# One layer with a state-space scan and a routed feed-forward: another order inside the inner layer's banks, a margin for ScalarE, and one name set right

## The chip, the cores and the metric

The kernel runs on one core of a Trainium2 chip. Its engines are TensorE (matmuls and transposes, PE; its weight loads are shown as PEld), VectorE (DVE), ScalarE (ACT), GpSimd (POOL) and SyncE (SP, which issues the transfers here). Each engine works through its own queue in the order of the program, and waits at an instruction until its operands are ready. The metric is the device time of one execution in microseconds; lower is better.

## What is computed

Input u has 4 sequences of 2048 tokens with 256 features. All arithmetic is in float32.

```
x = u + ssm(layernorm(u))
out = x + ffn(layernorm(x))

ssm: u_in = v @ W_in.T + b_in; x, z = halves (512 channels each)
     delta, B, C from x @ W_x.T (rank 16, 16 states, 16 states); delta = softplus(delta @ W_dt.T + b_dt)
     h[t] = h[t-1] * exp(delta[t] * A) + x[t] * delta[t] * B[t]       per channel and state
     y[t] = sum over states of h[t] * C[t];  y = (y + x * D) * silu(z);  y @ W_out.T + b_out

ffn: scores = softmax(v @ Wg.T + bg) over 4 experts, the best two are kept, with weights w
     h_e = relu(v @ Wi.T + low-rank part of expert e)       (1024 features)
     out = sum over the two of w_e * (h_e @ Wo.T)
```

## The kernel before

The 8192 tokens are cut into 16 chunks of 512. For a chunk there are 512 channels in 4 blocks of 128 and 16 states, so 64 scans of a 128x512 tile; 1024 scans in all are the backbone of the program. One scan takes:

- on ScalarE a decay `dA = exp(delta * a)`, made two scans ahead, and a small copy of the last column (`carry`) for the next chunk;
- on GpSimd `dBx = xdt * B` for two states at once, four scans ahead (`xdt` is delta times x);
- on VectorE the scan itself (a tensor_tensor_scan), and a product `hC = h * C`. For every fourth scan this product is made on GpSimd and called `hP`;
- on TensorE four transposes that add `hC` into the bank of y.

Everything else is put between the scans: the front of the next chunk (layer norm, projections `pin`, `pdbc`, `pdt`, their copies `xT`, `dbc`, `delta`, the softplus over delta, then `xdt`), the gate (`g`, a silu), the output projection of the last chunk (`po`), and the last chunk's feed-forward, here called the inner layer.

The inner layer of a chunk has 8 halves k (4 token blocks, 2 halves of 512 features). A half has one PSUM bank `pz`. Two matmuls with x2T (`p_base`, line 661; four records in the profile) give the part that all experts share. `p_low` (line 670) adds the low-rank part: in one step, the second slot's part of half k, and the first slot's of half k-1. The first slot's operand is the difference of the two experts' masks, so it turns the bank from one expert to the other. `a_relu` (line 681) reads the bank twice, first with slot 1 and then, after the next `p_low`, with slot 0, and gives the bank back. `p_hT` transposes and sums the two relus, ScalarE copies `hT`, and `p_down` (`pf`) projects it down.

The order is not written out by hand. `Pacer` (line 45) holds threads of `Step`s. A step has an engine, a cost in us, the steps it comes after, and PSUM banks that it takes or gives back (three banks in all, for everything but y and dA). The pacer keeps a planned time for each engine. After each scan and after each read, `fill` (line 106) writes out the side steps that are `ready` (line 126). For ScalarE a step is ready when its planned start is at most 0.6 us after VectorE's planned time and its end at most 1.5 us, or when it could have begun 0.5 us earlier. `force` (line 147) writes a step, and all it needs, at once; the main loop does so at deadlines. After the last scan `drain` (line 138) writes what is left, in order of planned start.

`front` gives back a chunk's `xdts`, the steps that make delta times x. The first chunk's are named `xdts` in line 897. In the main loop line 954 sets the same name to the next chunk's; line 952 uses it at scan 27.

All instructions are recorded through a helper in line 30, so the profile names line 30 for nearly all of them; the tiles' names tell them apart.

Of the kernel before, what the change touches and what calls it, by code (L numbers as in the profile page):

```python
# [44 lines left out]
class Pacer:  # L45
# [80 lines left out]
    def ready(self, x):  # L126
        t = self.start(x)
        if t is None:
            return False
        v = self.now["dve"]  # L130
        if self.quiet and x.engine == "act" and x.cost > self.MOST:
            return False
        if x.engine == "dve":
            t = max([y.end for y in x.after if y.engine != "dve"], default=0.0)
            return t + self.LATENCY + self.MARGIN <= v
        return t <= v + self.BEGIN[x.engine] and (t + x.cost <= v + self.END[x.engine] or t <= v - 0.5)

    def drain(self):
# [30 lines left out]
def ssm_moe_layer_kernel(  # L169
# [100 lines left out]
    bm_sb = const.tile([32 * TOPK, F], F32, tag="bm_sb", name="bm_sb")  # L270
# [18 lines left out]
    def mm_tile(name):  # L289
        return ps.tile([P, TC], F32, tag="mm", name=name)  # L290

    pe, act, dve, pool = (InOrder(tc, e) for e in (nc.tensor, nc.scalar, nc.vector, nc.gpsimd))
    pacer = Pacer(BANKS)
# [83 lines left out]
    def new_xnT(c):  # L377
        st[c]["xnT"] = chunk.tile([P, KM, TC], F32, tag="xnT", name=f"xnT_{c}", bufs=1)
        return st[c]["xnT"]
# [5 lines left out]
    def front_norm(c):  # L385
        def load():
            if c + 1 < NCHUNK:
                us[c + 1] = load_u(c + 1, "ua")

        return layernorm_T(lambda: us[c], lambda: new_xnT(c), f"a{c}", Step("sp", 5.0, load))  # L390
# [167 lines left out]
    def ffn(c):  # L558

        s = st[c]  # L560
        q = {}
# [96 lines left out]
        HF = F // 2  # L658
        NK = 2 * NJ

        def p_base(k):
            j, half = divmod(k, 2)
            pm = q["z", k] = mm_tile(f"pz_{c}_{k}")
            for m in range(KM):
                pe.matmul(
                    pm, lhsT=s["x2T"][:, m, j * P : (j + 1) * P], rhs=wi_sb[:, m, half * HF : (half + 1) * HF],
                    start=(m == 0), stop=False, skip_group_check=True,
                )

        def p_low(k):  # L670
            for slot, x in ((1, k), (0, k - 1)):
                if 0 <= x < NK:
                    j, half = divmod(x, 2)
                    r = slice(32 * slot, 32 * slot + ER)
                    pe.matmul(
                        q["z", x], lhsT=s["lowT"][r, j * P : (j + 1) * P],
                        rhs=bm_sb[r, half * HF : (half + 1) * HF], start=False, stop=True,
                        skip_group_check=True,
                    )

        def a_relu(k, slot):
            h = q["h", k, slot] = work.tile([P, HF], F32, tag=f"h{slot}", name=f"h{slot}_{c}_{k}")
            act.activation(h, q["z", k], AF.Relu, scale=s["topv"][:, slot, k // 2 : k // 2 + 1])
# [36 lines left out]
        steps = layernorm_T(lambda: s["u"], lambda: new_x2T(c), f"f{c}")  # L720
# [14 lines left out]
        last = steps[-1]  # L735
        for x in steps[-3:]:
            x.after = [steps[steps.index(x) - 1]] + held.get("low", [])
        z1s, hs, copies = [], [], []
        bases = [Step("pe", 1.75, lambda k=k: p_base(k), after=[last], takes=1) for k in range(NK)]
        steps.append(bases[0])  # L740
        for k in range(NK + 1):

            low = Step(
                "pe", 1.06 if 0 < k < NK else 1.05, lambda k=k: p_low(k), after=bases[k : k + 1] + z1s[-1:]
            )
            steps.append(low)
            if k:
                hs.append(Step("act", 0.57, lambda k=k: a_relu(k - 1, 0), after=[low], gives=1))
                steps.append(hs[-1])
            if k < NK:  # L750
                z1s.append(Step("act", 0.57, lambda k=k: a_relu(k, 1), after=[low]))
                steps.append(z1s[-1])
            steps += bases[k + 1 : k + 2]
            if k:
                steps.append(Step("pe", 0.88, lambda k=k: p_hT(k - 1), after=[hs[-1]], takes=1))
                steps.append(Step("act", 0.5, lambda k=k: a_hT(k - 1), after=[steps[-1]], gives=1))
                copies.append(steps[-1])
            for j in range(NJ):
                if k == min(2 * j + 3, NK):
                    for h in range(2):  # L760
                        steps.append(
                            Step("pe", 1.75, lambda j=j, h=h: p_down(j, h), after=[copies[2 * j + 1]], takes=1 - h)
                        )
                    steps.append(Step("dve", 0.33, lambda j=j: add(j), after=[steps[-1]], gives=1))
# [6 lines left out]
    def load_bc(i, h):  # L771
# [11 lines left out]
    states = [  # L783
        (c, (c * NH + hf) * NG + g, hf * ND2 + dd, g * NN + k)
        for c in range(NCHUNK) for hf in range(NH) for g in range(NG) for dd in range(ND2) for k in range(NN)
    ]
# [107 lines left out]

    spare = small.tile([P, 1], F32, tag="spare", name="spare", bufs=1)
    act.activation(spare, mhalf[:, 0:1], AF.Softplus)
    f, g, dbc, xdts = front(0, front_norm(0))
    pacer.add(f)
    pacer.force(f[2 * NJ])
    join_x()  # L900
# [4 lines left out]
        load_bc(i, 0)  # L905
    for i in range(2):
        load_bc(i, 1)
    pacer.force(xdts[0])

    act.activation(a_sb, a_sb, AF.Exp)  # L910
    dve.tensor_scalar_mul(a_sb, a_sb, -1.0)
    pacer.add(g)
    for i in range(0, AHEAD_B, NN):
        pacer.force(xdts[states[i][2]])
        X[i] = X[i + 1] = pacer.run("pool", 2.32, lambda: enter(i))
    for i in range(AHEAD_A + 1):
        A[i] = pacer.run("act", 0.63, lambda: decay(i))
# [6 lines left out]
    for i in range(M + 4):  # L924

        pacer.quiet = (i + 5) % (PER // NH) < 8
        if turn:
            pacer.run("pe", 0.45, *turn)
            turn = None
        for e in (1, 4):  # L930

            if i + e < M + 3 and i + e >= 3:
                c, _, d, n = states[i + e - 3]
                c2, d2 = (c + 1, d - ND2) if d >= ND2 else (c, d + ND2)
                if n == N - 1 and e == (1 if d % ND2 else 4) and c2 < NCHUNK:
                    scale, x = open_y(c2, d2)
                    xds[c2, d2] = x, [pacer.run("act", 0.63, scale)]
        if 3 <= i < M + 3:
            c, _, d, n = states[i - 3]
            if n == N - 1:  # L940
                copy, *steps = close_y(c, d)
                pacer.force(silus[c])
                steps[0].after = [pacer.run("act", 0.5, copy, [Y[i - 3]]), silus[c]]
                pacer.add(steps, first=True)
                gates.setdefault(c, []).append(steps[-1])
                turn = xds.pop((c + 1, d - ND2) if d >= ND2 else (c, d + ND2), None)
                if d == ND - 1:
                    begin(c + 1)
        if i < M:
            at = i % PER  # L950
            if i == PER // NH - AHEAD_B - 1:
                pacer.force(xdts[-1])
            if states[i][0] + 1 in deadline:
                dbc, xdts = deadline[states[i][0] + 1]
                if at == PER - 3 * NN * ND2 - 2:
                    pacer.force(dbc)
                if at == PER - AHEAD_B - 6:
                    pacer.force(xdts[0].after[0])
                if at == PER - AHEAD_B - 1:
                    pacer.force(xdts[-1])  # L960
            S[i] = pacer.run("dve", 1.2 if states[i][0] % CPB else 1.14, lambda: scan(i), [A[i], X[i]])
        if i + AHEAD_B < M and i % NN == 0:
            X[i + AHEAD_B] = X[i + AHEAD_B + 1] = pacer.run(
                "pool", 2.32, lambda: enter(i + AHEAD_B), [S[i - 1]]
            )
        pacer.fill()

        if 1 <= i <= M:
            if shared(i - 1):
                C[i - 1] = pacer.run("pool", 1.23, lambda: read(i - 1), [S[i - 1]])  # L970
            else:
                C[i - 1] = pacer.run("dve", 0.6, lambda: read(i - 1), [S[i - 1], *summed[-4:-3]])
            pacer.run("act", 0.1, lambda: keep(i - 1), [(S if shared(i - 1) else C)[i - 1]])
            if i + AHEAD_A < M:
                A[i + AHEAD_A] = pacer.run(
                    "act", 0.63, lambda: decay(i + AHEAD_A), [(S if shared(i - 1) else C)[i - 1]]
                )
        for late in (3, 2):
            if late <= i < M + late and (late == 3) == shared(i - late):
                Y[i - late] = pacer.run("pe", 0.45, lambda: sum_y(i - late), [C[i - late]])  # L980
                if late == 2:
                    summed.append(Y[i - late])
        if i < M:
            group(i)
        pacer.fill()
# [48 lines left out]
```

## Time and profile before

| | us |
|---|---|
| median of 3 runs | 2129.7 (2126.46 to 2132.01) |
| profiled execution | 2129.43 |
| its span | 2127.7 |
| VectorE busy | 1855.8 |
| TensorE busy | 1873.9 |
| GpSimd busy | 1709.4 |
| ScalarE busy | 1441.7 |
| mean granted TensorE clock | 0.929 |

The span is the time from the first to the last instruction of the profiled execution; 1.7 us of its time lie around it. A row of a group or of the timeline gives line, engine, operation, output<-inputs and shape; a number in square brackets, with an arrow, is the idle time of the engine just before and what ended it. Some matmul records can be missing, and a group of matmuls overlaps with the next by the pipeline, so that its time is a little longer than from start to start.

### The profile page before, as it was taken

How to read it: one execution, taken by the hardware profiler on the slowest of the kernel's cores; microseconds unless marked ns; L12 is line 12 of the kernel's file. 1: busy time of each engine (PE TensorE's matmuls, PEld its weight loads, DVE VectorE, ACT ScalarE, POOL GpSimd, SP SyncE). 2: the span in 40 equal slices, each digit the busy share in tenths (PEclk: the TensorE clock that was granted, in tenths of full speed). 3: DMA queues.
4: the chain of work that ended last, by engine and by line, in shares of the span. 5: the costliest groups of instructions: out<-in, count | busy, mean ns of one | idle time of the engine just before them, and what ended most of it. 6: DMA issues, size and time to landing. Idle time of an engine off the chain costs nothing.

```text
span 2127.7 us, 28591 instructions
## 1 busy us (share of the span) xinstructions
PE 1873.9 (88%) x9504; PEld 1284.0 (60%) x9504; DVE 1855.8 (87%) x2423; ACT 1441.7 (68%) x2898; POOL 1709.4 (80%) x1084
## 2 busy tenths in 40 slices
PE   7768788998889989899899988989899998989978
PEld 4445555665566665657666565766657575666655
DVE  4899898999989989999989998999989999999810
ACT  5857667667676667676767777676677867766522
POOL 5898888989878878888888888888888888878600
PEclk9859799998999999999999999999999999989989
DMA  7454344445444443434435454444535444444200
GB/s 218 144 165 152 127 150 149 149 147 161 151 139 151 149 140 138 169 130 149 163 130 164 140 167 132 147 152 139 169 130 173 136 141 149 138 149 140 98 10 10
DMA packets 106132, 300.70 MB, mean 141 GB/s; under 512 B 12864, under 2 KB 39104, under 8 KB 105984
## 3 DMA queue, kind: packets, MB, share of 16 engines
q1 hardware_dynamic: 105984, 298.88, 42.8%
q8 instruction: 74, 1.21, 0.2%
q14 instruction: 74, 0.61, 0.1%
HBM read 289.41 MB, written 9.44 MB: 140 GB/s over the span
## 4 chain that ended last, share of the span: by engine, by line
PE 25%; DVE 20%; ACT 12%; issue 5%; POOL 1%; DVEq 0%; POOLq 0%; ACTq 0%
DVE dA L30 9%; PE pz L30 9%; PE y L30 5%; PE pf L30 5%; ACT dA L30 5%; DVE hC L30 4%; DVE hS L30 4%; PE phT L30 3%; ACT L30 2%; ACT h L30 1%; PE pin L30 1%; ACT delta L30 1%; ACT g L30 1%; DVE u L30 1%; DVE plg L30 1%
## 5 line engine op out<-in xcount | busy, mean ns | idle before, releaser
L30 POOL TENSOR_TENSOR dBx<-xdt,B 128x1024 f32<-128x1024 f32 x512 | 1207.8, 2363 | 187.5 <-DVE dA L30 157.3
L30 ACT ACTIVATE dA<-delta,a_sb 128x512 f32<-128x512 f32 x1024 | 706.8, 693 | 143.0 <-DVE hC L30 66.8
L30 DVE TENSOR_TENSOR_SCAN dA<-dA,carry,dBx 128x512 f32<-128x512 f32 x576 | 726.4, 1279 | 62.6 <-ACT dA L30 51.0
L30 PE MATMUL y<-ident,hC 128*128 128x128 f32 x3072 | 490.7, 291 | 36.6 <-DVE hC L30 36.5
L30 DVE TENSOR_TENSOR hC<-dA,C 128x512 f32<-128x512 f32 x768 | 514.1, 670 | 0.2 <-issue 0.2
L30 PEld LDWEIGHTS y<-ident,hC 128*128 128x128 f32 x3072 | 386.1, 150 | 181.3 <-issue 73.6
L30 POOL TENSOR_TENSOR hP<-hS,C 128x512 f32<-128x512 f32 x256 | 326.6, 1276 | 5.1 <-issue 4.1
L30 PE MATMUL pz<-wi_sb,x2T 128*128 128x512 f32 x512 | 271.7, 657 | 25.2 <-ACT hT L30 15.4
L30 DVE TENSOR_TENSOR_SCAN dA<-dA,dBx 128x512 f32<-128x512 f32 x192 | 231.2, 1220 | 35.3 <-ACT dA L30 30.5
L30 DVE TENSOR_TENSOR_SCAN hS<-dA,carry,dBx 128x512 f32<-128x512 f32 x192 | 244.1, 1271 | 18.6 <-ACT carry L30 10.6
L30 PE MATMUL pf<-wo_sb,hT 128*128 128x256 f32 x1024 | 243.4, 383 | 11.6 <-ACT hT L30 9.4
L30 PE MATMUL pin<-xnT,w_in_sb 128*128 128x512 f32 x512 | 245.9, 612 | 5.5 <-ACT g L30 3.6
L30 ACT COPY carry<-dA 128x1 f32<-128x1 f32 x576 | 90.1, 157 | 208.5 <-DVE hC L30 206.5
L30 ACT ACTIVATE h<-pz,topv 128x512 f32<-128x512 f32 x256 | 165.4, 680 | 74.1 <-PE pz L30 73.4
L30 PEld LDWEIGHTS pf<-wo_sb,hT 128*128 128x128 f32 x1024 | 186.5, 190 | 41.6 <-ACT hT L30 14.4
L30 PEld LDWEIGHTS y<-ident,hP 128*128 128x128 f32 x1024 | 128.3, 148 | 96.3 <-issue 56.7
L30 PE MATMUL y<-ident,hP 128*128 128x128 f32 x1024 | 167.1, 288 | 18.7 <-POOL hP L30 18.7
L30 PEld LDWEIGHTS pz<-wi_sb,x2T 128*128 128x128 f32 x512 | 95.2, 207 | 124.9 <-issue 76.2
L30 PE MATMUL pz<-bm_sb,lowT 16*128 16x512 f32 x512 | 167.9, 660 | 0.0
L30 PE MATMUL phT<-ident,h 128*128 128x128 f32 x1024 | 139.7, 281 | 21.3 <-ACT h L30 16.8
L30 PEld LDWEIGHTS pin<-xnT,w_in_sb 128*128 128x128 f32 x512 | 92.3, 197 | 93.1 <-issue 75.2
L30 PEld LDWEIGHTS phT<-ident,h 128*128 128x128 f32 x1024 | 120.8, 145 | 44.2 <-ACT h L30 19.5
(94 smaller groups left out, 1784.8 us busy)
## 6 DMA issues: line engine op xcount, KB each, us to landing
B<-bc SPq DMA_DIRECT2D x256, 512.0 KB, 3.7
C<-bc SPq DMA_DIRECT2D x256, 512.0 KB, 3.7
ua<-in_u_dram SPq DMA_DIRECT2D x16, 512.0 KB, 5.5
u<-in_u_dram SPq DMA_DIRECT2D x16, 512.0 KB, 4.4
out_dram<-u SPq DMA_DIRECT2D x16, 512.0 KB, 4.8
w_in_sb<-in_w_inT_dram SPq DMA_DIRECT2D x2, 512.0 KB, 4.7
wi_sb<-in_wiT_dram SPq DMA_DIRECT2D x1, 1024.0 KB, 6.7
wo_sb<-in_woT_dram SPq DMA_DIRECT2D x1, 1024.0 KB, 10.4
```

The source lines that it names most:

```text
L30: return self._tc.keep_in_program_order(f(*args, **kwargs))
```

## The change

Three things are changed.

- In the inner layer a bank is begun by the second slot's low-rank part (`start=True`), then the base is added, then the relu of slot 1 reads it; the first slot's part still comes last. `p_low` of half k takes the bank, `p_base` of half k comes after it, and the relu of slot 1 comes after the base.
- A ScalarE step that comes after a TensorE step whose planned end is close is ready only when ScalarE's planned time has reached that end (and that end plus 0.5 us lies at most 0.6 us after VectorE's planned time). For such a step the rule on its own end no longer applies.
- The first chunk's `xdts` have a name of their own, `first_xdts`, and line 952 uses that.

```diff
@@ Pacer.ready
             return t + self.LATENCY + self.MARGIN <= v
+        if x.engine == "act" and any(y.engine == "pe" and y.end + 0.5 > t for y in x.after):
+            t = max(y.end for y in x.after) + 0.5
+            return t <= v + self.BEGIN["act"] and self.now["act"] + 0.5 >= t
         return t <= v + self.BEGIN[x.engine] and (t + x.cost <= v + self.END[x.engine] or t <= v - 0.5)
@@ p_base
-            pm = q["z", k] = mm_tile(f"pz_{c}_{k}")
+            pm = q["z", k]
...
-                    start=(m == 0), stop=False, skip_group_check=True,
+                    start=False, stop=True, skip_group_check=True,
@@ p_low
                 if 0 <= x < NK:
+                    if slot:
+                        q["z", x] = mm_tile(f"pz_{c}_{x}")
...
-                        rhs=bm_sb[r, half * HF : (half + 1) * HF], start=False, stop=True,
+                        rhs=bm_sb[r, half * HF : (half + 1) * HF], start=bool(slot), stop=not slot,
@@ ffn
-        bases = [Step("pe", 1.75, lambda k=k: p_base(k), after=[last], takes=1) for k in range(NK)]
-        steps.append(bases[0])
+        bases = []
...
-                "pe", 1.06 if 0 < k < NK else 1.05, lambda k=k: p_low(k), after=bases[k : k + 1] + z1s[-1:]
+                "pe", 1.06 if 0 < k < NK else 1.05, lambda k=k: p_low(k), after=[last] + z1s[-1:], takes=int(k < NK)
...
             if k < NK:
-                z1s.append(Step("act", 0.57, lambda k=k: a_relu(k, 1), after=[low]))
-                steps.append(z1s[-1])
-            steps += bases[k + 1 : k + 2]
+                bases.append(Step("pe", 1.75, lambda k=k: p_base(k), after=[low]))
+                z1s.append(Step("act", 0.57, lambda k=k: a_relu(k, 1), after=bases[-1:]))
+                steps += [bases[-1], z1s[-1]]
@@ start and main loop
-    f, g, dbc, xdts = front(0, front_norm(0))
+    f, g, dbc, first_xdts = front(0, front_norm(0))
...
-    pacer.force(xdts[0])
+    pacer.force(first_xdts[0])
...
-        pacer.force(xdts[states[i][2]])
+        pacer.force(first_xdts[states[i][2]])
...
             if i == PER // NH - AHEAD_B - 1:
-                pacer.force(xdts[-1])
+                pacer.force(first_xdts[-1])
```

## The prediction

> **What bounds the kernel now.** I read the page's busy shares first, then busy time by stage, then VectorE's waits, then single stretches in order of time.
>
> ```profile
> PE 1873.9 (88%) x9504; PEld 1284.0 (60%) x9504; DVE 1855.8 (87%) x2423; ACT 1441.7 (68%) x2898; POOL 1709.4 (80%) x1084
> ...
> 43.00:151.00 108.00, 75.33 (x321) 48.50 (x319) 96.81 (x115) 74.91 (x156) 96.45 (x56) 0.73 0.49 160
> ...
> 647.00:2015.00 1368.00, 1250.23 (x6515) 863.80 (x6514) 1271.66 (x1654) 969.25 (x1960) 1164.57 (x733) 0.95 0.44 146
> 2015.00:2054.00 39.00, 37.69 (x182) 26.69 (x180) 5.07 (x10) 9.86 (x16) 0.00 (x0) 1.00 0.04 14
> 2054.00:2072.00 18.00, 6.47 (x25) 5.14 (x26) 4.79 (x22) 4.41 (x11) 3.11 (x10) 0.56 0.00 0
> 2072.00:2128.00 56.00, 49.58 (x196) 28.34 (x196) 1.70 (x4) 15.51 (x25) 0.00 (x0) 0.96 0.03 10
> ```
>
> The columns of a stage are span, PE, PEld, DVE, ACT and POOL busy, granted clock, DMA share, GB/s. From 43 to 2015 the 1024 scans run: VectorE is the fullest engine (1271.66 of 1368 in the long stage). From 2015 no scan is left and TensorE alone works: that is the drain, 113 us. So the time is the scan stream plus the drain, and the stream can shrink only by VectorE's idle time. What it waits for between 43 and 2015:
>
> ```profile
> DVE dA L30 <- ACT dA L30: 79.6, 128, 6.1
> DVE hS L30 <- ACT carry L30: 21.0, 10, 6.5
> DVE hS L30 <- ACT dA L30: 7.8, 8, 1.5
> ```
>
> Nearly all is ScalarE (108.4 us in these three rows): a decay exp(delta*a) comes late, because something stood ahead of it in ScalarE's queue. ScalarE's own waits in the same window say what:
>
> ```profile
> ACT hT L30 <- PE phT L30: 61.9, 62, 3.9
> ACT h L30 <- PE pz L30: 40.7, 53, 3.7
> ```
>
> ScalarE has slack (969 of 1368 busy), so it is the order of its queue that hurts. I went through every VectorE gap of 0.3 us or more in the stream, looking at the last ScalarE instructions before it. They sum to 118 us: 56 us behind a pack with two table loads (softplus or silu), 39 us behind a copy or relu that waited for TensorE (h, hT, xT, g, delta and the like), 14 us behind the copies of y and the next chunk's xd, 9 us other. Three of the packs stand out; this is the longest, VectorE's gap and ScalarE meanwhile:
>
> ```profile
> 626.72 1.22 DVE L30 TENSOR_TENSOR_SCAN hS<-dA,dBx 128x512 f32<-128x512 f32 x1 [6.45 <-ACT carry L30]
> ```
>
> ```profile
> 620.08 1.27 ACT L30 ACTIVATE delta<-pdt,b_dt_sb 128x512 f32<-128x512 f32 x2 [1.25 <-PE pdt L30]
> 621.36 1.28 ACT L30 ACT_TABLE_LOAD   x1
> 622.65 1.91 ACT L30 ACTIVATE delta<-delta 128x2048 f32<-128x2048 f32 x1
> 624.47 0.14 ACT L30 COPY carry<-dA 128x1 f32<-128x1 f32 x1
> 624.63 1.28 ACT L30 ACT_TABLE_LOAD   x1
> ```
>
> Four delta copies, a wait and the softplus pack stand between two decays. Gaps of this kind: 6.07 (89.99), 6.45 (626.72) and 3.60 us (754.77).
>
> **The change, part by part.** The number of instructions, of table loads (64) and of transfers is the same; only the order differs. I read it from both programs, counting by scan.
>
> (a) The first chunk's xdts. Line 954 sets the name xdts to the second chunk's steps from scan 0 on, so line 952 at scan 27 does not find the first chunk's, and forces the whole front of chunk 1. That is the 6.07 us gap. In the changed program nothing is forced at 27, and that softplus stands at scan 36. The gaps at 626.72 and 754.77 are forces at deadlines (scans 310 and 374); in the changed order no force does anything any more after the start, since the softplus of those chunks comes at scan 35 and 26 of the chunk, in place of 54. All 31 softplus and silu packs then have the ordinary size: pack, one carry, one decay, 5.3 us of ScalarE work, against 7.4, 8.0 and 6.7 for the three forced ones (copies times their rows). A softplus that is not forced cost VectorE 0.6 us in the mean over 12 chunks (0 to 2.3). Gain: 6.07 + 6.45 + 3.60 - 3 x 0.6 = 14 us. Ends: 7 (each ends up beside a silu pack, which costs some 2 us) and 16. The silu packs stay (about 2 us each, 31 us).
>
> (b) The margin. A step after a TensorE step is now put into ScalarE's queue only when ScalarE's planned time has reached the planned end. In the changed order a relu stands 1.57 scans behind its matmul in the mean, before 1.16; a copy of hT 1.71, before 1.12; xT and g 1.56, before 0.92. One scan with its read and its share of side work is 1972 / 1024 = 1.93 us, so they come 0.8 to 1.2 us later. The gaps they cause are 39 us in some 40 pieces, about 0.9 us each: by size alone most would go. Not all: the longest ScalarE waits are 3.7 and 3.9 us, and what waits behind a later relu is the bank and the next low-rank step. What is late next is the copy of y, which is not asked with a margin (14 us stays), and the packs. Ends: 32 saved, and a loss of 20 (rival below). By the size of the pieces I would take 23.
>
> Here a rule of the Trainium skill stands against the change. The row first: low-rank matmuls take 1.13 us for a group of four, and 2.08 at 1072.77, just ahead of a relu that waited 1.46 us and a VectorE gap of 1.64; a base group took 1.98 us in the drain, and 3.62 at 2072.75 after 18 us at a granted 0.56. "TensorE: Matmul & The Clock Gate" (Part 1, the HAM clock gate) says that the array goes to half speed after an idle window of about 3.4 us and needs as long a busy one to come back. The long stage's 0.95 is then 10% of its time at half speed, 43 to 151 at 0.73 more than half. Until now the first relu of a bank waited for the low-rank pair, which half speed makes 0.95 us longer; from now on it waits for the base group, 1.6 us longer, and the margin is 0.5. By the rows at full clock the sum has 23; by the rule, 10% of 120 first relus lose up to 0.7 us more, 8 us on ScalarE, of which perhaps a third reaches VectorE. I take 20.
>
> (c) The bank. Before: base(k+1) ran while relu 1 of bank k ran. After: low(k), base(k), hT(k-1), low(k+1); low(k+1) needs relu 1 of k (0.69 us, and 0.18 from the matmuls' end to the relu, as at 2019.36 and 2019.54 in the drain), and hT(k-1), 0.96 us, lies in between. Cost in the stream: nothing, covered by hT; without that cover 0.9 us per bank. Behind a low(k+1) that waits stand, on TensorE, the sums of y, which free VectorE's four hC buffers; VectorE's read waited 0.2 us in all before, so two or three scans of delay there cost nothing. On POOL and SP the moved steps are xdt (1.27 us each, 4 per chunk), the layer norms' small steps and one load of u (5.5 us to land, asked a chunk ahead): they move with their fronts by some ten scans, and VectorE waited 3.9 us for POOL in the whole stream. I take nothing for them, 5 us without that cover.
>
> (d) The drain. Because everything of chunk 14's inner layer comes later, more of it is left: in the changed order 7 bases instead of 3, 8 hT groups instead of 5, 7 low groups instead of 5, 8 half down-projections instead of 6. In rows (start to start in the drain): 4 x 1.82 + 3 x 0.96 + 2 x 1.05 + 2 x 1.82 = 15.9 us of TensorE. Not all of it lengthens the path. Before the layer norm of chunk 15 stand 7 bases (12.7), 6 low (6.3), 7 hT (6.7), py (1.7), two down pairs (7.3) and po (7.0): 41.7 us against the 35.3 from 2018.3 to 2053.6, +6.4; the rest (a down pair, low 8, hT, the last down pair) now fills the 18 us in which TensorE had 6.47 busy, and lengthens those by perhaps 1.5 (relu 8 ahead of xn, a half down-projection ahead of the routing). The last sums of y no longer stand behind a down pair (2012.90 to 2016.62): -1.6. The last inner layer begins with the low-rank part, so its base is not under the copy of lowT: +1.82, less the 1.0 to 1.5 that before lost at other waits: +0.5. Sum +6.8, ends 2 and 14.
>
> Sum against the profiled execution (span 2127.7, 1.7 us around it, 2129.4; the median of the runs is 2129.7, the same): -14 - 20 + 7 = -27, so 2102.5 us.
>
> **The rivals.**
> Half gain. The packs, not TensorE, set ScalarE's lateness, and the waits only move to the copies of y: (a) 9, (b) 8, (d) +11: 2123.5. For it: 56 us of packs and 14 of y stay. Against: the order by scans moves every kind of step.
> Slower: the first relu now waits for the base. Place: relu 1 of 120 banks. If TensorE is later than planned (hC sums take 0.60 to 0.66 us in the rows, planned 0.45), each such relu waits 0.5 us longer and half reaches VectorE, (b) turns into +30: -14 + 30 + 7 = 2152; with 0.3 us, +18, 2140. It decides from +7, that is 0.06 us per relu on VectorE; 2136 and more need 0.12. For it: ScalarE waits 40.7 us for pz already. Against: relus stand 0.4 scan later.
> The change doesn't do what it says: that nothing is forced any more is seen in the order, so (a) is only open in size, and this has little weight.
>
> **How the numbers follow.** A run of this kernel can tell some 0.3%, 6.4 us, from no change. Forecast 0.60 (2085 to 2115), half gain 0.20 (2115 to 2130), slower 0.20 (2130 to 2152). Faster by over 0.3% (below 2123.3): 0.60 and half of half gain, 0.70. Same: the other half and a tenth of the slower case, 0.12. Slower: 0.18. Lowest end: -16 - 32 + 2 = -46, 2083. Range 2080 to 2140: the low end with a little below it, the high end into the slower case at 0.3 us per relu.
>
> **What would show it.** Right: no VectorE gap over 4 us behind a softplus; ScalarE's waits for pz and phT in the stream below 60 us together (102.6 before); VectorE idle in the stream down by 25 to 40; the last scan at about 1980 and a drain of about 120 us. Wrong: ScalarE's wait for pz grows, or the drain grows by over 15 us, or VectorE waits for sums of y (hC <- PE).

## The result, and the profile after

The changed kernel takes 2111.0 us (median of 4 runs, 2109.3 to 2111.8) against 2130.6 (4 runs, 2126.5 to 2132.0): a ratio of 0.991, 95% interval 0.990 to 0.992. It is faster by 19.6 us, three times the 6.4 us that the prediction took as the least that can be told. The forecast was 2102.5, so 8.5 us of the forecast gain are missing. The profiled execution took 2109.27 us, its span is 2107.5.

The same stages as before, cut where the new execution has its edges. The first row is the page's, the others are busy time by stage (span, PE, PEld, DVE, ACT and POOL busy, granted clock, DMA share, GB/s):

```profile
PE 1860.5 (88%) x9504; PEld 1266.0 (60%) x9504; DVE 1852.9 (88%) x2423; ACT 1440.0 (68%) x2898; POOL 1707.3 (81%) x1084
...
43.00:151.00 108.00, 75.75 (x328) 49.55 (x326) 99.95 (x118) 75.73 (x158) 100.76 (x58) 0.70 0.50 169
647.00:1984.00 1337.00, 1213.27 (x6365) 832.93 (x6366) 1255.02 (x1631) 954.76 (x1925) 1150.26 (x723) 0.95 0.45 148
1984.00:2031.00 47.00, 46.52 (x212) 29.67 (x211) 4.82 (x10) 15.48 (x24) 0.00 (x0) 0.99 0.00 0
2031.00:2049.00 18.00, 12.70 (x67) 9.39 (x65) 5.23 (x24) 5.31 (x13) 3.10 (x10) 0.93 0.09 30
2049.00:2108.00 59.00, 53.36 (x193) 29.92 (x192) 1.70 (x4) 16.26 (x25) 0.00 (x0) 0.88 0.03 9
```

VectorE works as long as before, and the scans end at 1984 instead of 2015. The first drain stage is 47 us and was 39, TensorE full in both; the 18 us of the layer norm and routing now hold 12.70 us of TensorE's work, before 6.47; the last stage is 59 for 56, at a granted 0.88 for 0.96. From the first scan's start to the last one's end the stream went from 1983.2 to 1952.4 (-30.8), the drain from 112.9 to 123.4 (+10.5).

What VectorE waits for in the stream (its three largest rows), then ScalarE's waits for `pz` and `phT`, whose rows of before stand in the prediction (total, times, longest; us):

```profile
DVE dA L30 <- ACT dA L30: 71.6, 122, 2.4
DVE hS L30 <- ACT carry L30: 13.9, 12, 2.3
DVE dA L30 <- ACT carry L30: 7.5, 6, 3.1
```

```profile
ACT h L30 <- PE pz L30: 40.2, 56, 3.0
...
ACT hT L30 <- PE phT L30: 4.0, 13, 0.6
```

The longest wait of VectorE for a decay or a carry is 3.1 us, where three forced packs made 6.45, 6.07 and 3.60. ScalarE's wait for `phT` fell from 61.9 to 4.0 us. The one for `pz` did not fall at all: 40.7 before, 40.2 now. That is the first thing to explain.

VectorE's gaps of 0.3 us and more in the stream (all but the one ahead of the first scan), put down to the last things that ScalarE did before each, as in the prediction, beside the drain (us). A pack is a softplus or silu with its two table loads; PE-fed steps are copies and relus that waited for TensorE. Where several of these stand before one gap the class is a choice: another count of the last instructions moves the entries of before and of the changed kernel by up to 3 us, those of E3 to E5 by up to 7. Sums and drains don't depend on it.

| kernel | packs | PE-fed steps | copies of y, xd | other | sum | drain |
|---|---|---|---|---|---|---|
| before | 56.3 | 38.6 | 14.2 | 8.7 | 117.8 | 112.9 |
| after | 42.2 | 20.8 | 17.9 | 10.5 | 91.4 | 123.4 |
| before + name (E1) | 51.5 | 31.1 | 14.6 | 9.4 | 106.6 | 112.9 |
| before + margin (E2) | 53.2 | 11.9 | 10.1 | 19.7 | 94.9 | 130.8 |
| before + bank order (E3) | 60.7 | 58.0 | 14.1 | 8.2 | 141.0 | 102.4 |
| after - bank order (E4) | 50.0 | 7.4 | 10.1 | 22.4 | 89.9 | 131.0 |
| after - margin (E5) | 56.6 | 59.0 | 14.3 | 8.2 | 138.1 | 102.4 |
| after - name (E6) | 47.9 | 20.7 | 18.4 | 10.5 | 97.6 | 119.7 |

### The profile page after: what moved, and what is told of

It reads as the page before. It is cut to its first block, busy times and chain, and to the rows that moved or that the text cites. A ratio compares the mean times of both kernels' runs of the same rounds, so it can differ in the third digit from the quotient of the medians.

```text
span 2107.5 us, 28645 instructions
## 1 busy us (share of the span) xinstructions
PE 1860.5 (88%) x9504; PEld 1266.0 (60%) x9504; DVE 1852.9 (88%) x2423; ACT 1440.0 (68%) x2898; POOL 1707.3 (81%) x1084
## 5 line engine op out<-in xcount | busy, mean ns | idle before, releaser
L30 PE MATMUL y<-ident,hC 128*128 128x128 f32 x3072 | 484.7, 289 | 64.7 <-DVE hC L30 64.3
L30 PEld LDWEIGHTS y<-ident,hC 128*128 128x128 f32 x3072 | 380.6, 149 | 218.2 <-DVE hC L30 94.8
L30 PE MATMUL pz<-wi_sb,x2T 128*128 128x512 f32 x512 | 267.3, 648 | 0.0
L30 DVE TENSOR_TENSOR_SCAN dA<-dA,dBx 128x512 f32<-128x512 f32 x192 | 231.5, 1220 | 22.4 <-ACT dA L30 14.2
L30 ACT ACTIVATE h<-pz,topv 128x512 f32<-128x512 f32 x256 | 173.2, 680 | 111.0 <-PE pz L30 108.1
L30 PE MATMUL pz<-bm_sb,lowT 16*128 16x512 f32 x512 | 176.7, 671 | 33.5 <-ACT carry L30 10.5
```

The costliest lines, as they stand in the source:

```text
L30: return self._tc.keep_in_program_order(f(*args, **kwargs))
```

## The experiments

Every ratio is against the kernel before, run on the same chip, with its 95% interval. The experiments ran on four chips, on which the kernel before took 2128.5 to 2130.7 us, so they are compared with the changed kernel by ratio (0.001 is 2.1 us). Streams, drains and rows are those of one profiled execution of each kernel.

**E1, E2, E3: one part alone.** E1 is before with the name alone:

```diff
-    f, g, dbc, xdts = front(0, front_norm(0))
+    f, g, dbc, first_xdts = front(0, front_norm(0))
...
-                pacer.force(xdts[-1])
+                pacer.force(first_xdts[-1])
```

> The kernel before with the name first_xdts alone. Theory (each forced softplus pack costs its gap of VectorE less that of an ordinary pack): the 6.07 us gap at scan 27 shrinks to about 1 to 2 us, the silu two scans later keeps its 2 us, everything from chunk 1 on is as before: 4 to 5 us less than before, the two deadline gaps (6.45 and 3.60 us) still there. Rival (the pack costs the same wherever it stands): within 1 us of before.

E2 is before with the three lines of the margin alone:

```diff
+        if x.engine == "act" and any(y.engine == "pe" and y.end + 0.5 > t for y in x.after):
+            t = max(y.end for y in x.after) + 0.5
+            return t <= v + self.BEGIN["act"] and self.now["act"] + 0.5 >= t
```

> The kernel before with ScalarE's margin alone. Theory (the margin takes the waits for TensorE out of ScalarE's queue and pays in the drain): ScalarE's wait for phT in the stream falls from 62 us to below 10, VectorE's gaps behind such waits lose about 20 us, the drain holds 15 bases of the inner layer (11 before) and is 10 to 13 us longer; forces at scans 27, 246 and 502 stay: sum 5 to 12 us less than before. Rival (the bank's order brings the gain): no faster than before, or slower by the 10 us of the drain.

E3 is before with the bank order alone:

```diff
-            pm = q["z", k] = mm_tile(f"pz_{c}_{k}")
+            pm = q["z", k]
...
-                z1s.append(Step("act", 0.57, lambda k=k: a_relu(k, 1), after=[low]))
+                bases.append(Step("pe", 1.75, lambda k=k: p_base(k), after=[low]))
+                z1s.append(Step("act", 0.57, lambda k=k: a_relu(k, 1), after=bases[-1:]))
```

> The kernel before with the bank begun by the low-rank part alone, without the margin and without the new name. In the program's order the deadline forces at scans 310 and 374 are gone, and 10 bases are left for the drain (11 before). Theory (margin brings the smaller waits, the bank the smaller packs): the two deadline gaps go (8 us), ScalarE's waits for pz and phT stay near 100 us or grow since the relus now wait for the base: 3 to 10 us less than before. Rival (a relu that waits for the base loses more than the packs give): 5 to 15 us more than before, ScalarE's wait for pz well above 41 us.

Measured: name 0.996 (0.994 to 0.997), margin 0.993 (0.992 to 0.995), bank order 1.002 (1.002 to 1.003). The name gained 9 us where 4 to 5 were expected (the last section comes back to it), the margin 14 where 5 to 12 were. The bank order alone makes the kernel slower, as its rival said, and does so in spite of a drain that is 10.5 us shorter: its stream is 18.4 us longer (2001.6). ScalarE's waits in the stream of E3, the same two rows:

```profile
ACT h L30 <- PE pz L30: 105.4, 101, 3.7
...
ACT hT L30 <- PE phT L30: 6.1, 11, 0.9
```

The wait for `phT` goes without any margin (61.9 to 6.1): by the new order of the steps ScalarE has the relu behind the base to do ahead of that copy. The wait for `pz` grows by 65 us: the first relu has moved behind the base. One of them in E3, TensorE first, then ScalarE, then VectorE in the same 10 us:

```profile
1903.18 2.07 PE L30 MATMUL pz<-bm_sb,lowT 16*128 16x512 f32 x2
1905.18 3.75 PE L30 MATMUL pz<-wi_sb,x2T 128*128 128x512 f32 x4
```

```profile
1909.03 0.69 ACT L30 ACTIVATE h<-pz,topv 128x512 f32<-128x512 f32 x1 [2.91 <-PE pz L30]
...
1909.65 0.71 ACT L30 ACTIVATE dA<-delta,a_sb 128x512 f32<-128x512 f32 x1
```

```profile
1910.45 1.29 DVE L30 TENSOR_TENSOR_SCAN dA<-dA,carry,dBx 128x512 f32<-128x512 f32 x1 [2.92 <-issue]
```

The base takes 3.75 us (1.98 at full clock), the relu stands in ScalarE's queue for 2.91, the decay behind it begins at 1909.65, and VectorE stands for 2.92. The row says `issue`, but the scan begins as that decay ends. This is the mechanism of the prediction's slower rival, and without the margin it decides the sign. Sorted by the matmul that ended last before the relu, 80.7 us of E3's waits for `pz` end with a base, 47.4 of them in 15 waits at half clock; before, all ended with a low-rank group.

E2 shows the opposite trade: the stream falls by 29.2 us (to 1954.0), the PE-fed gaps from 38.6 to 11.9, and the drain grows by 17.9. The margin delays the inner layer of chunk 14, and what is delayed is left for the drain: 15 groups of base matmuls after the last scan, before 11.

**E4, E5, E6: the changed kernel less one part** (the diffs above, turned round).

> The changed kernel with the bank as before (base first), margin and new name stay. From the parts measured alone (new name 9 us less, margin 15 us less, bank 4 us more) theory A, the parts add up, gives 2107, some 4 us faster than the changed kernel. Theory B, the bank needs the margin (with it the relus stand late enough behind the base, and the order without forces is the bank's), gives a slower one than the changed kernel: 2113 to 2118, with a drain of about 130 us (123 in the changed kernel) that is not made good in the stream.

> The changed kernel without the margin (bank and new name stay). Theory (the margin is worth some 20 us of VectorE's gaps in the stream and costs about 10 in the drain): stream 15 to 25 us longer than in the changed kernel, drain 10 to 14 us shorter: 5 to 12 us slower than the changed kernel, so about 2117 to 2123. Rival (the margin takes no net time, the packs were all): equal to the changed kernel or faster, 2100 to 2111.

> The changed kernel with the old name for the first chunk's xdts; bank and margin stay. Theory (the force at scan 27 is a pack of 7 to 8 us in ScalarE's queue and costs its gap): a VectorE gap of 5 to 7 us at scan 27 is back, chunk 0 is 4 to 6 us longer, all later chunks as in the changed kernel: 4 to 6 us slower, about 2116. Rival (what the first chunk gains is lost in the next ones, as between the two kernels without the margin, which differed by under 1 us): within 2 us of the changed kernel.

Measured: without the bank order 0.994 (0.993 to 0.996), without the margin 1.002 (1.001 to 1.003), without the name 0.992 (0.991 to 0.994), against 0.991 (0.990 to 0.992) for all three. The whole gain hangs on the margin: taken out, the kernel is slower than before (2134.3 us, where 2117 to 2123 were expected), with `pz` waits of 113.3 us. The name can't be told from nothing once the other two are there, as E6's rival said, but for another reason: in the profiled executions E6's stream is 5.8 us longer (1958.2), and its drain 3.8 us shorter (E8 says why). The bank order, a loss alone, is a gain of 0.3% beside the margin, since the intervals of E4 and the changed kernel stand apart.

Where that gain is: not in the stream (1950.7 in E4, 1952.4 in the changed kernel), but in the drain, 131.0 against 123.4, with 15 bases after the last scan in both. In E4 all of that work stands ahead of the last layer norm: in the 18 us of layer norm and routing TensorE is busy for 6.4 us, as before, in the changed kernel for 12.5. In the stream the base-first order waits far less. E4, the same two rows:

```profile
ACT h L30 <- PE pz L30: 7.0, 16, 1.7
ACT hT L30 <- PE phT L30: 6.5, 10, 1.7
```

So 33 of the 40 us of `pz` waits that remain in the changed kernel come from the bank order. I split ScalarE's waits of over 0.3 us for TensorE's results, those of the y bank left out, by the clock granted 1 us before each wait ended (us; ahead of the bar at half clock):

| kernel | half clock / full clock | half clock's share of the stream |
|---|---|---|
| before | 31.4 / 134.0 | 0.141 |
| E2, margin | 4.8 / 36.5 | 0.111 |
| E3, bank order | 69.6 / 131.5 | 0.179 |
| E4, margin, base first | 2.0 / 33.2 | 0.109 |
| after | 25.1 / 27.1 | 0.138 |

At full clock the margin takes away three quarters of the waits in either order. At half clock it does so only where the relu waits for the low-rank pair; where it waits for the base, 25 us stay. The moment by which a wait is dated is a choice: from its start to its end the changed kernel's half-clock part goes from 28 to 14 us, E4's stays below 2. Of the relus of the changed kernel alone, 10 waited for a base at half clock, for 20.3 us in all. Such a place looks like this (TensorE, ScalarE, VectorE; a base takes 1.98 us at full clock):

```profile
1541.65 3.33 PE L30 MATMUL pz<-wi_sb,x2T 128*128 128x512 f32 x4
...
1545.02 0.69 ACT L30 ACTIVATE h<-pz,topv 128x512 f32<-128x512 f32 x1 [2.11 <-PE pz L30]
...
1546.43 0.71 ACT L30 ACTIVATE dA<-delta,a_sb 128x512 f32<-128x512 f32 x1
...
1547.23 1.23 DVE L30 TENSOR_TENSOR_SCAN dA<-dA,dBx 128x512 f32<-128x512 f32 x1 [3.06 <-ACT carry L30]
```

**E7: the margin only as long as its delay can be made up.** If the margin of the last chunks only filled the drain, taking it away from scan 928 on should gain.

```diff
+        pacer.late = i < 928
...
-        if x.engine == "act" and any(y.engine == "pe" and y.end + 0.5 > t for y in x.after):
+        if self.late and x.engine == "act" and any(y.engine == "pe" and y.end + 0.5 > t for y in x.after):
```

> The changed kernel with the margin only up to scan 928 of 1024. Theory (the margin pays in the drain, since the last inner layers lag): 12 bases are left for the drain in place of 15, the drain is 8 to 12 us shorter, the last one and a half chunks lose 3 us each: 3 to 8 us faster than the changed kernel, 2103 to 2108. Rival (the drain's length is set by the last layer alone, which is serial): drain within 3 us, time 0 to 5 us longer.

Measured 0.993 (0.992 to 0.995): no gain, rather some 5 us lost, though the interval just meets that of the changed kernel. The drain fell by 5 us (118.4), but the stream is 9.6 us longer, 8.9 of it in the last 64 scans (128.9 us instead of 120.0). This theory fell: in these executions the margin is worth more in the last chunk than it costs in the drain.

**E8: is the last stage longer by the clock?** In the changed kernel TensorE stands idle just before the last inner layer:

```profile
2041.61 1.97 PE L30 MATMUL pf<-wo_sb,hT 128*128 128x256 f32 x8
2048.15 1.06 PE L30 MATMUL plT<-ident,lowm 128*64 128x128 f32 x4 [4.56 <-POOL lowm L30]
2049.88 2.07 PE L30 MATMUL pz<-bm_sb,lowT 16*128 16x512 f32 x2 [0.67 <-ACT lowT L30]
2051.88 3.78 PE L30 MATMUL pz<-wi_sb,x2T 128*128 128x512 f32 x4
2055.59 2.98 PE L30 MATMUL pz<-bm_sb,lowT 16*128 16x512 f32 x4
2058.50 3.78 PE L30 MATMUL pz<-wi_sb,x2T 128*128 128x512 f32 x4
```

E8 fills the gap with 36 transposes of the identity, whose result nothing reads:

```diff
+            for j in range(36 if c == NCHUNK - 1 else 0):
+                pe.transpose(pl[:, (j % NJ) * P : (j % NJ + 1) * P], ident, ident)
```

> The changed kernel with 36 extra transposes of the identity on TensorE in the last chunk, between the routing and the transposes of the low-rank part, where TensorE is idle for 4.6 us; nothing reads them. Theory (the idle window sends TensorE to half clock, and the last inner layer starts with it): the first low-rank groups and bases of the last layer take 1.1 and 2.0 us in place of 2.1 to 3.0 and 3.8, the granted clock in the last 60 us is above 0.97, drain 3 to 5 us shorter: about 2107. Rival (half clock comes from something other than that gap): the rows of the last layer as in the changed kernel, time equal or up to 1 us longer.

```profile
2043.77 4.09 PE L30 MATMUL plT<-ident 128*128 128x128 f32 x36
2048.50 0.63 PE L30 MATMUL plT<-ident,lowm 128*64 128x128 f32 x4 [0.64 <-POOL lowm L30]
2049.79 1.12 PE L30 MATMUL pz<-bm_sb,lowT 16*128 16x512 f32 x2 [0.67 <-ACT lowT L30]
2050.84 1.98 PE L30 MATMUL pz<-wi_sb,x2T 128*128 128x512 f32 x4
```

The low-rank pair falls from 2.07 to 1.12 us and the base from 3.78 to 1.98, with the same operands. From 2048 to the end, the stage row of the changed kernel and then of E8:

```profile
2048.00:2107.50 59.50, 54.21 (x196) 30.46 (x196) 1.70 (x4) 16.26 (x25) 0.09 (x1) 0.87 0.03 9
```

```profile
2048.00:2101.30 53.30, 47.69 (x196) 27.94 (x196) 1.70 (x4) 16.30 (x25) 0.44 (x2) 0.99 0.03 10
```

The same 196 matmul records take 47.69 us instead of 54.21, at 0.99 instead of 0.87. Measured 0.988 (0.987 to 0.990), 2104.4 us, some 6 us below the changed kernel, though the two intervals just meet. So the idle 4.56 us cost some 6 us more through the clock. "TensorE: Matmul & The Clock Gate" of the Trainium skill (Part 1) tells of this, half speed after an idle window of about 3.4 us; here the gap is 4.56 us, and the same rows are seen at both speeds in one pair of kernels.

What such a gap costs is not fixed. E6 has the same 4.56 us ahead of the same work, but there half clock ends sooner: the second low-rank group and base take 2.03 and 1.98 us (2.98 and 3.78 in the changed kernel), and from `plT` to the end it needs 56.0 us at a granted 0.93, the changed kernel 59.3 at 0.87. That is 3.3 of the 3.8 us by which E6's drain is shorter. No run shows what sets the end of half clock there. The other half of the rule that the prediction quotes, a busy window as long to come back, is not borne out: in the changed kernel TensorE works without a gap from 2049.88 on, and the base at 2058.50 still takes 3.78 us.

**E9: the work of the longer drain put where it is covered.** In the drain, steps go out by planned start (`drain`, line 138). E9 lets everything that is not inner layer go 0.5 us ahead, so that the last chunk's own chain starts sooner and chunk 14's inner layer fills its holes:

```diff
-            x, thread = min(heads, key=lambda h: self.start(h[0]))
+            x, thread = min(heads, key=lambda h: self.start(h[0]) - (0.5 if self.of.get(id(h[1])) != "inner" else 0.0))
```

> The changed kernel with one more line: in the drain a step that is not of an inner layer goes ahead of one of the inner layer that could start at the same planned time (half a us of preference). The last output projection (po) then comes right after the last sums of y, the layer norm of the last chunk runs beside the inner layer of chunk 14, and the rest of that layer lies in the stretch in which TensorE was idle. Theory (after the last scan TensorE's work, done without holes and at full clock, sets the end; the three holes and the half clock are what the drain can give back): drain 107 to 112 us against 123, the base rows of the last layer near 2.0 us, time 2094 to 2100. Rival (the drain is a serial chain of the last layer, and what fills the holes delays it): drain 120 us or more, time 2108 or more.

Measured 0.984 (0.983 to 0.985), 2095.4 us, the stream unchanged (1952.5), the drain 109.9. Its TensorE at the places that matter:

```profile
1992.48 3.72 PE L30 MATMUL po<-w_out_sb,g 128*128 128x256 f32 x16
...
2031.08 1.86 PE L30 MATMUL plg<-wga_sb,x2T 128*128 128x20 f32 x16
2032.79 3.70 PE L30 MATMUL pf<-wo_sb,hT 128*128 128x256 f32 x16
...
2039.00 0.63 PE L30 MATMUL plT<-ident,lowm 128*64 128x128 f32 x4
```

The output projection starts at 1992.48, some 9 us after the last scan. Behind the routing (`plg`) down-projections and transposes of chunk 14 fill what was the 4.56 us hole, and `plT` takes 0.63 us and not 1.06: full clock. By parts, the time between the last scan and plT's start goes from 64.1 to 55.2 us, and from there to the end from 59.3 to 54.6.

**E10: E9 with the base first.** This asks whether the bank order still pays once the drain is ordered so.

> The same preference in the drain, with margin and new name, and the bank as before (base first). Theory A (with the margin the bank's new order gave its gain over the old one only in the drain, where base first holds a bank longer and py and po come late): stream equal to the other within 4 us, drain equal within 3 us, so time within 3 us of the run with the new bank. Theory B (the new bank order is better in the drain in itself): drain 5 to 8 us longer than that run's.

Measured 0.988 (0.987 to 0.990), 2104.6 us: the stream is 4 us shorter (1948.4), the drain 14.6 longer (124.5), where theory B had 5 to 8 and theory A nothing. TensorE has as much left to do after the last scan as in E9 (15 bases, 16 transposed pairs `hT`, 16 half down-projections), and 13.9 of the 14.6 us lie between the end of `po` and `plT`: there TensorE is idle for 7.3 us (0.6 in E9), at a granted 0.87 (1.00 in E9). Some of its rows there:

```profile
2006.02 3.72 PE L30 MATMUL pf<-wo_sb,hT 128*128 128x256 f32 x16 [0.68 <-ACT hT L30]
...
2034.47 1.94 PE L30 MATMUL phT<-ident,h 128*128 128x128 f32 x8 [4.42 <-DVE m L30]
2036.34 2.07 PE L30 MATMUL pz<-bm_sb,lowT 16*128 16x512 f32 x4
```

With the base first nothing lies between the transposes and the down-projection, which then waits 0.68 us for its copy (twice in this stretch); and the work of chunk 14 that is left is placed such that a hole of 4.42 us stands behind the routing, and the transposes behind it take 1.94 us and not 1.04. That the bank order itself, and not this one placing of the work, brings the hole is not shown.

**E11: half the margin**, E9 with 0.25 in the place of each 0.5 of the margin.

> The run with the preference in the drain and the new bank, with a margin of 0.25 us in place of 0.5. Theory (it is asking at the planned end at all that takes the waits away, the size matters little): ScalarE's waits for pz and phT in the stream grow by less than 15 us, time within 3 us of the run with 0.5. Rival (the size covers the time by which TensorE's real ends lie behind the planned ones): waits grow by more than 25 us and the time by 5 us or more.

Measured 0.987 (0.986 to 0.989), 2103.2 us, 8 more than E9, all in the stream (1961.1). ScalarE's waits at half clock go from 21.6 to 36.7 us, at full clock from 33.0 to 27.6. So the size counts, and it counts where half clock makes a base longer. The theory had the waits right (`pz` and `phT` together grew by 12.3 us, less than its 15), the rival the time.

**E12: each order where it is good.** The base first for chunks 0 to 13, which lie in the stream, the new order for 14 and 15, with E9's drain:

```diff
+        turned = c >= NCHUNK - 2
...
-        bases = []
+        bases = [] if turned else [Step("pe", 1.75, lambda k=k: p_base(k), after=[last], takes=1) for k in range(NK)]
...
+                if turned:
+                    bases.append(Step("pe", 1.75, lambda k=k: p_base(k), after=[low]))
+                    steps.append(bases[-1])
```

> The run with the preference in the drain and a margin of 0.5, where only the inner layers of the last two chunks begin their banks with the low-rank part; the other 14 begin with the base as before. Theory (with the margin the new bank order gives its gain in the drain alone, and in the stream it costs some waits at half clock): stream as in the run with base first and the same preference (1948, against 1952 with the new order everywhere), drain 108 to 112 us, so 2090 to 2095, up to 5 us faster than the new order everywhere. Rival (the new order is worth something in the stream too): stream longer than 1955 or time above 2098.

Measured 0.983 (0.981 to 0.984), 2092.1 us: the fastest here, some 17 us below the changed kernel. The stream is 1945.7, the drain 112.1, ScalarE waits at half clock 2.6 us in all. Its interval overlaps that of E9 (0.983 to 0.985), so that it beats the changed kernel is shown, that it beats E9 is not.

## Why the prediction was right, and where it was off

Most of the forecast gain came, and from the margin, as forecast. That the sum lies so near is in part luck: term (a) has the right size for a reason that holds only in part, and in (d) errors of up to 3 us stand beside opposite ones of up to 2.

By the profiled executions: predicted -27.2 us of span, seen -20.2. The stream lacks 3.2 us of its forecast gain (-34, seen -30.8), the drain is 3.7 us longer than forecast (+6.8, seen +10.5).

**(a) The name and the forced packs, -14.** The class measures -14.1 (56.3 to 42.2). The size is right, but the reason given covers only a part. The gap at scan 27 is the name's doing, as said. E6, which lacks only the name, has it back, and the changed kernel has 2.13 us at that softplus:

```profile
89.54 1.23 DVE L30 TENSOR_TENSOR_SCAN dA<-dA,dBx 128x512 f32<-128x512 f32 x1 [6.84 <-ACT dA L30]
```

```profile
102.53 1.23 DVE L30 TENSOR_TENSOR_SCAN dA<-dA,dBx 128x512 f32<-128x512 f32 x1 [2.13 <-ACT carry L30]
```

The packs of E6 and of the changed kernel differ by 5.7 us, their first chunks by 4.1 (118.5 and 114.4 us long). The other two forced packs were taken for a matter of the margin's new order. But E1 still has both (6.45 and 3.60 us), and E2 and E4 still have one (5.43 and 5.42). They go when the bank order is there: of the gaps over 3 us behind a softplus E3 has only that at scan 27 (6.28), E5 none. Without the margin that brings little, since a softplus that is not forced then costs 1.3 us in the mean and not 0.6: E5 loses 19.1 us to its 15 softplus, before 24.1, the changed kernel 8.6. The 0.6 for an ordinary one, taken from before, held only with the margin. The silu packs, said to stay at about 31 us, measure 33.6.

**(b) The margin, -20.** PE-fed gaps fell by 17.8. Right in kind and nearly in size. Half clock was charged too little: 12 first relus at 0.7 us, 8 us on ScalarE, were reckoned; 10 waited, for 20.3 us. What of that reaches VectorE is not settled. With the base first (E4) the class is 7.4 instead of 20.8, but E4 has 12 us more in "other" and 8 more in packs, against 8 less in the copies; a forced pack of 5.42 us is among these, the rest stays open. In the whole stream the runs with the base first are shorter by 1.7 us (E4), 4.1 (E10) and 6.8 (E12). The copies of y, named as what is late next, took 3.7 us more, not charged.

**(c) The bank order at nothing in the stream.** True only beside the margin: 1.7 us between E4 and the changed kernel. Without it 18.4 (E3). The prediction named `hT`'s 0.96 us as the cover, for 0.9 us per bank; what the runs show is that the base itself is what the relu waits for, and that the cover is the time by which the margin moves the relu. The slower rival had both the place and the mechanism, and is kept out by the margin alone. That its +18, reckoned with the margin, is near E3's 18.4, without it, is chance.

**(d) The drain, +6.8.** This is the term that was mis-sized. Of its +10.5: up to the last y's end +1.7 (forecast -1.6), to the end of po +5.8 (+6.4), layer norm and routing -0.4 (+1.5), last inner layer +3.6 (+0.5). The work left over ahead of the layer norm was right to 0.6 us. Two things were not. I took the sums of y to end sooner since no down pair stands ahead of them, and they end later. And for the last layer the step "+1.82, less the 1.0 to 1.5" left half clock as it was before, where it covered one base (3.62 us); now it covers two bases and two low-rank groups. E8 and E9 show that it is the clock: at full clock that part takes 52.8 and 54.6 us instead of 59.3, below the 55.8 of before. How long half clock lasts there is not the order's doing alone: E6, the same but for the name, needs 56.0 us, so that part of this miss is chance.

Of the signs named: no gap over 4 us behind a softplus, seen; waits for pz and phT below 60, seen (44.2); VectorE's idle time down by 25 to 40, seen (26.4 in gaps of 0.3 us and more); last scan and drain at about 1980 and 120, 1984 and 123.4. Of the counter-signs none: the wait for pz did not grow, the drain grew by less than 15 us, and no row of `hC` waiting for PE appears.

## What to carry to other kernels

A margin on an in-order queue trades waits in the steady part against work left at the end: count both, and then give the end an order of its own, since one line for the tail (E9) brought some 15 us where the whole change had brought 19.6. An order that is right in the steady part can be wrong in the tail and the other way round (E10: stream 4 us shorter, drain 14.6 longer), so try it by place (E12). And test a part both alone and taken out: the bank order is a loss of 0.24% alone and a gain of 0.3% in company, and the name gains 0.4% alone, about half of it by its own order (next section), and nothing that can be told in company.

## What had not been expected of the hardware

Filling 4.56 us of TensorE's idle time with 4.09 us of useless transposes shortened what stands behind it by some 6 us (E8): the 196 records there ran at 0.99 and not 0.87 of the clock.

Half clock is not spread evenly over waits: in the changed kernel it covers 14% of the stream and makes nearly half of ScalarE's waits for these results (25.1 of 52.2 us), while with the base first (E4) 11% of the stream makes 2.0 of 35.2.

The same order of instructions does not always take the same time. From chunk 1 to chunk 14 each engine runs the same instructions in the same order before and in E1. Of the 10.6 us by which E1's stream is shorter, 4.6 are in chunk 0 and the name's; the other 6 come with an order that is the same. What differs is the clock: half clock covers 280 us of the stream before and 252 in E1. In chunk 9 it covers 10.2 us before (124.5 us long) and nothing in E1 (121.4 us). The runs' times fit this: four of E1's five took 2118.9 to 2119.7 us at a granted 0.932 to 0.935, the fifth 2125.7 at 0.924, some 5 us below before, which lies at 0.925 to 0.930. So of the name's 9 us about half is the order that was changed, and a change of a few us in this stream can be the clock's. Why half clock falls elsewhere is not settled.
